# Weights of a pairwise bilinear kernel read as rows 248 KiB apart instead of contiguous blocks

## Chip, cores and metric

One core of one Trainium2 chip. The metric is device time in microseconds (us), as the median of repeated runs. KB in the profile's issue lists means 1024 bytes; the rows "254 KB apart" of the change are 253,952 bytes, 248 KiB.

## The reference

For each of the 496 pairs (i, j) of 32 fields, the vector of field i is multiplied by that pair's 128 x 128 matrix, and the result is multiplied element by element with field j.

```python
v_i = inputs[:, I_IDX, :]                 # [1024, 496, 128]
v_j = inputs[:, J_IDX, :]
transformed = jnp.einsum('bpd,ped->bpe', v_i, W)     # W: [496, 128, 128]
return transformed * v_j                  # 260 MB of float32
```

## The kernel before

Each pair has two halves of 512 batch columns. TensorE makes the product in PSUM. For all but the first 15 pairs it takes three float32r matmuls on split operands, with a scaling by ScalarE in between; ScalarE and GpSimd split the weights shortly ahead of use. VectorE multiplies by field j into one of four output buffers of two pairs each, and SyncE's queue stores the buffer as 1 MB with rows of 8 KB. The same queue loads weights, four pairs at a time, and x.

```python
WL = 4                      # pairs per weight load
WLEAD = 4                   # loads ahead
rpool = ctx.enter_context(tc.tile_pool(name="wr", bufs=5))     # raw weights
opool = ctx.enter_context(tc.tile_pool(name="o", bufs=4))      # output, 2 pairs each
...
def load_x(f, n=1, pieces=1, eng=None):
    ...
        (eng or nc.sync).dma_start(out=t[:, :, k * s : (k + 1) * s], in_=xt[:, f : f + n, k * s : (k + 1) * s])
...
def load_w(c, splits=(0, WL)):
    w_raw[c] = rpool.tile([P, WL, P], F32, tag="w", name=f"w_{c}")
    for a, b in zip(splits, splits[1:]):
        nc.sync.dma_start(out=w_raw[c][:, a:b, :], in_=wt[c, :, a:b, :])
...
for u in range(2 * NQ + LAG):           # half pairs
    q = u // 2
    if u % (2 * WL) == 0 and (q // WL + WLEAD) * WL < NQ:
        load_w(q // WL + WLEAD)
    ...                                  # matmuls of u, product and store of u - LAG, splits ahead
...
xt = _np.ascontiguousarray(x.transpose(2, 1, 0))                       # [d, field, b]
wt = _np.ascontiguousarray(w[perm].reshape(NQ // WL, WL, P, P).transpose(0, 3, 1, 2))
```

## Time and profile before

| | kernel before |
|---|---|
| time, median (first three runs) | 768.28 us (766.63 to 769.2) |
| span of the profiled run | 769.8 us |
| TensorE / ScalarE / VectorE / GpSimd busy | 722.7 / 638.7 / 632.0 / 593.2 us |
| DMA engines, main queue | 99.4% of 16 engines' span |
| output / x / weights moved | 260.0 / 16.8 / 32.5 MB |
| packets of 8 / 4 / 2 KB, main queue | 31,616 / 3,840 / 16,256 |

Read this table from the bottom. A DMA packet is here one row of one partition. If the recorded times of all packets, divided by 16, add up to the span, the engines have hardly any idle time, and then it is the packet count times the packet duration that must be asked about. The mean of a packet group minus its median is its tail: stalls of single packets. The lines themselves are in the prediction.

### The profile page before, as it was taken

To read this page: it belongs to the slowest core of one execution; us is meant where nothing else is said; L and a number is where in the kernel's file an instruction comes from. 1 tells how busy PE (TensorE), PEld (TensorE's weight loads), DVE (VectorE), ACT (ScalarE), POOL (GpSimd) and SP (SyncE) were. 2 spreads that over 40 slices of the span, in tenths; PEclk is the share of its full clock that TensorE was granted. 3 is DMA by queue.
4 is the path that set the end of the run, shared out by engine and by line. 5 is a ranking of instruction groups with operands and counts; after the bars stand their busy time and mean duration, and the time that the engine had idled before them with its cause. 6 is when DMAs were issued, how large, how long until landed. Compare 5 with 4: busy or idle time off the path is not lost.

```text
span 769.8 us, 11824 instructions
## 1 busy us (share of the span) xinstructions
PE 722.7 (94%) x2946; PEld 545.4 (71%) x2946; DVE 632.0 (82%) x1012; ACT 638.7 (83%) x1256; POOL 593.2 (77%) x863
## 2 busy tenths in 40 slices
PE   7988999999999999999999989999999999999994
PEld 3556766677777676777777767777777777777773
DVE  4869888888888788888888878888888888888885
ACT  2276988888888898888888889998988898998983
POOL 2677998887889878878878696978786969697660
PEclk9999999999999999999999999999999999999998
DMA  9999999999999999999999999999999999999997
GB/s 352 424 419 384 407 397 410 405 400 406 410 405 403 400 409 416 409 379 421 411 414 407 412 403 406 411 407 408 415 410 395 408 410 409 409 408 405 400 401 307
DMA packets 59108, 310.11 MB, mean 403 GB/s; under 512 B 6560, under 2 KB 6816, under 8 KB 27424
## 3 DMA queue, kind: packets, MB, share of 16 engines
q1 hardware_dynamic: 58464, 308.31, 99.4%
q10 hardware_dynamic: 576, 1.05, 0.4%
q8 instruction: 24, 0.39, 0.2%
q14 instruction: 44, 0.36, 0.1%
HBM read 49.28 MB, written 260.05 MB: 402 GB/s over the span
## 4 chain that ended last, share of the span: by engine, by line
DMA 61%; DVE 21%; PE 15%; issue 2%; DVEq 0%; SPq 0%; ACT 0%
DMA out_dram<-ot 60%; DVE ot L172 19%; PE po L157 9%; PE po L166 4%; DVE xd L195 2%; PE po L154 1%; DMA x<-in_xt_dram 1%; DVEq L172 0%; SPq L85 0%; DVEq L217 0%; ACT po L158 0%; DVEq L195 0%
## 5 line engine op out<-in xcount | busy, mean ns | idle before, releaser
L172 DVE TENSOR_TENSOR ot<-po,x 128x512 f32<-128x512 f32 x992 | 618.6, 684 | 129.5 <-DMA out_dram<-ot 70.2
L158 ACT ACTIVATE po<-po 128x512 f32<-128x512 f32 x962 | 551.2, 583 | 106.5 <-PE po L157 53.3
L157 PE MATMUL po<-xh,wh 128*128 128x512 f32 x962 | 388.7, 404 | 24.4 <-DVE ot L172 21.6
L166 PE MATMUL po<-xd,wd 128*128 128x512 f32 x962 | 376.9, 392 | 5.7 <-DVE xd L195 5.7
L157 PE MATMUL po<-xl,wl 128*128 128x512 f32 x962 | 377.6, 392 | 2.2 <-POOL wl L95 2.1
L157 PEld LDWEIGHTS po<-xh,wh 128*128 128x128 f32 x962 | 180.9, 188 | 110.2 <-DVE ot L172 72.5
L95 POOL TENSOR_TENSOR wl<-w,wh 128x256 fp32r<-128x256 f32 x241 | 179.2, 744 | 92.1 <-ACT wh L94 90.7
L166 PEld LDWEIGHTS po<-xd,wd 128*128 128x128 f32 x962 | 181.0, 188 | 46.3 <-ACT po L158 3.8
L157 PEld LDWEIGHTS po<-xl,wl 128*128 128x128 f32 x962 | 181.1, 188 | 36.8 <-POOL wl L95 4.5
L97 POOL TENSOR_TENSOR wd<-wl,wd 128x256 fp32r<-128x256 f32 x241 | 180.0, 747 | 20.1
L96 POOL TENSOR_SCALAR wd<-wh 128x256 fp32r<-128x256 f32 x241 | 99.1, 411 | 20.3
L94 ACT ACTIVATE wh<-w 128x256 fp32r<-128x256 f32 x241 | 99.2, 412 | 0.5 <-DMA w<-in_wt_dram 0.5
L110 POOL TENSOR_TENSOR xl<-x,xh 128x512 fp32r<-128x512 f32 x52 | 67.3, 1293 | 19.8 <-ACT xh L109 19.5
L115 POOL TENSOR_TENSOR xd<-xh,xl 128x512 fp32r<-128x512 f32 x32 | 41.4, 1292 | 2.7
L109 ACT ACTIVATE xh<-x 128x512 fp32r<-128x512 f32 x52 | 32.5, 628 | 10.5 <-DMA x<-in_xt_dram 10.3
L111 POOL TENSOR_SCALAR xl<-xl 128x512 fp32r<-128x512 f32 x52 | 32.8, 631 | 4.6
L154 PE MATMUL po<-x,w 128*128 128x512 f32 x60 | 29.0, 645 | 4.1 <-DMA x<-in_xt_dram 4.1
L154 PEld LDWEIGHTS po<-x,w 128*128 128x128 f32 x60 | 12.1, 206 | 20.2 <-issue 13.9
L195 DVE TENSOR_TENSOR xd<-xh,xl 128x512 fp32r<-128x512 f32 x20 | 16.6, 831 | 0.0
L109 ACT ACT_TABLE_LOAD x1 | 1.3, 1283 | 2.6 <-issue 2.6
L211 POOL MEMSET const-float32-0.0<- 128x1 f32 x1 | 0.1, 98 | 0.2 <-issue 0.2
L211 POOL MEMSET const-bfloat16-1.0<- 128x1 bf16 x1 | 0.1, 101 | 0.0
(2 smaller groups left out, 0.2 us busy)
## 6 DMA issues: line engine op xcount, KB each, us to landing
out_dram<-ot SPq DMA_DIRECT2D x247, 1024.0 KB, 8.9
w<-in_wt_dram SPq DMA_DIRECT2D x123, 256.0 KB, 9.1
x<-in_xt_dram SPq DMA_DIRECT2D x30, 512.0 KB, 9.5
x<-in_xt_dram ACTq DMA_DIRECT2D x4, 256.0 KB, 5.1
out_dram<-ot SPq DMA_DIRECT2D x4, 256.0 KB, 7.0
w<-in_wt_dram SPq DMA_DIRECT2D x1, 192.0 KB, 3.6
w<-in_wt_dram SPq DMA_DIRECT2D x1, 64.0 KB, 2.9
```

Of the source, the lines that this page charges most:

```text
L94: nc.scalar.mul(h, raw, 1.0 - 2.0**-13)
L95: nc.gpsimd.tensor_tensor(l, raw, h.bitcast(F32), ALU.subtract)
L96: nc.gpsimd.tensor_scalar(d, h.bitcast(F32), EPS, 1.0, ALU.mult, ALU.mult)
L97: nc.gpsimd.tensor_tensor(d, l.bitcast(F32), d.bitcast(F32), ALU.subtract)
L109: nc.scalar.mul(h, x_sb[f][:, s], 1.0 - 2.0**-13)
L110: nc.gpsimd.tensor_tensor(l, x_sb[f][:, s], h.bitcast(F32), ALU.subtract)
L115: nc.gpsimd.tensor_tensor(d, h.bitcast(F32), l.bitcast(F32), ALU.subtract)
L154: nc.tensor.matmul(po[u], w_raw[q // WL][:, q % WL, :], x_sb[i][:, s], start=True, stop=True)
L157: nc.tensor.matmul(po[u], w_s[c][t][:, r], x_s[i][t][:, s], start=t == 0, stop=t == 1)
L158: nc.scalar.mul(po[u], po[u], 1.0 + EPS)
L166: nc.tensor.matmul(po[u], w_s[q // WC][2][:, r], x_s[i][2][:, s], start=False, stop=True, skip_group_check=True)
L172: nc.vector.tensor_tensor(ots[g][:, k, s], po.pop(u), x_sb[j][:, s], ALU.mult)
```

## The change

The intent is a plain transposed layout [d, pair, e] on the host, in which a load may take any run of pairs. A load still takes four pairs, 2 KB per partition, but the 128 source rows, which lay end to end in 256 KB, now lie 248 KiB apart. The on-chip program keeps its order on all engines.

```diff
-            nc.sync.dma_start(out=w_raw[c][:, a:b, :], in_=wt[c, :, a:b, :])
+            nc.sync.dma_start(out=w_raw[c][:, a:b, :], in_=wt[:, c * WL + a : c * WL + b, :])
@@
-    wt = _np.ascontiguousarray(w[perm].reshape(NQ // WL, WL, P, P).transpose(0, 3, 1, 2))
+    wt = _np.ascontiguousarray(w[perm].transpose(2, 0, 1))
```

## The prediction

> **What bounds the kernel now.** I read the page's shares and slices first, then the queues, the chain of waits that ended last, a steady stretch of that chain, the waits, and last the single DMA packets of the trace, grouped by size. In the lines below, the slices give the busy tenths of the 16 DMA engines and what they moved.
>
> ```profile
> PE 722.7 (94%) x2946; PEld 545.4 (71%) x2946; DVE 632.0 (82%) x1012; ACT 638.7 (83%) x1256; POOL 593.2 (77%) x863
> ...
> DMA  9999999999999999999999999999999999999997
> ...
> q1 hardware_dynamic: 58464, 308.31, 99.4%
> ...
> HBM read 49.28 MB, written 260.05 MB: 402 GB/s over the span
> ...
> DMA 61%; DVE 21%; PE 15%; issue 2%; DVEq 0%; SPq 0%; ACT 0%
> ```
>
> TensorE looks busiest of the compute engines at 94%, but the DMA engines are full in every slice but the last, and one queue alone takes 99.4% of them. Of the 309 MB, 260 MB is output. The chain says the same: 61% of it is DMA, all but 1% the store of the output. A steady stretch of the chain shows how the kernel is paced:
>
> ```profile
> 589.45 8.95 DMA out_dram<-ot
> ...
> 598.52 2.50 DVE ot L172 x4
> ...
> 601.03 8.94 DMA out_dram<-ot
> ...
> 610.10 2.50 DVE ot L172 x4
> ```
>
> A store lands after 8.95 us, the output buffer is free, VectorE fills it with four products in 2.50 us, and it is stored again: one turn each 11.58 us (601.03 - 589.45). There are four such buffers, so one group of two pairs takes 11.58 / 4 = 2.90 us. Is that the DMA's own pace or mere latency? The packets answer. In the trace a packet of 8 KB (output rows) has a median of 309 ns, one of 4 KB (x rows) 159 ns, one of 2 KB (weight rows) 84 ns: 9 ns plus 75 ns for each 2 KB. The means are 319.7, 172.6 and 86.0 ns. A group's engine time is 8 output packets x 319.7 + 4 weight packets x 86.0 = 2558 + 344 = 2902 ns, which is the 2.90 us of the turn. And all packets of all queues add up to 770.4 us on each of 16 engines, against a span of 769.8. So the kernel is bound by DMA engine time: each nanosecond that a packet gets longer is paid in full.
>
> The loads of the weights themselves, and who waits for them:
>
> ```profile
> w<-in_wt_dram SPq DMA_DIRECT2D x123, 256.0 KB, 9.1
> ...
> x<-in_xt_dram SPq DMA_DIRECT2D x30, 512.0 KB, 9.5
> ```
>
> ```profile
> DVE ot L172 <- DMA out_dram<-ot: 70.2, 83, 2.1
> ...
> ACT wh L94 <- DMA w<-in_wt_dram: 0.5, 2, 0.3
> ```
>
> The last number of the first fence is the time from issue to landing in us; the waits are in total, times, longest. Nearly nobody waits for weights: 0.5 us in all. VectorE does wait for stores.
>
> **What the Trainium skill says.** "DMA: Bandwidth & Descriptors", section "Why a DMA increments its semaphore by 16 and not by 1": one descriptor moves one contiguous run of the last dimension, and a tile of 128 partitions is spread over 16 engines. The trace agrees: 123 weight loads of 256 KB make 123 x 128 = 15,744 packets of 2 KB, though the source was one contiguous block. Same page, "Latency and other measured facts", row on HBM row pitch at large powers of two: copies of [128 x 16 KiB] tiles ran at 207 GB/s per direction with a 512 KiB row pitch, 164 at 2 MiB, 103 at 4 MiB, and at 214 (called full) once the 4 MiB pitch was padded by 4 KiB; its mechanism, aliasing of HBM channels, is called an inference. The kernel before gives a partial test: x is already loaded as rows 128 KiB apart, a power of two. "HBM Reference", "Access": one core alone measures about 425 GB/s, bounded by its 16 DMA engines; here 8192 B in 309 ns on 16 engines is 424 GB/s. The same page, "Latency": 0.2 us on average and 2 us at high load; the longest 2 KB packet here took 1.63 us, so single slow reads exist.
>
> **The change part by part.** Removed: nothing that runs. The instruction order of all five engines is the same in both programs (the DMA queue's 405 entries too), and the built loads have the same destination, 128 rows of 512 elements; only the source step goes from 512 to 63,488 elements (253,952 B). The first block is still loaded in two pieces of 512 B and 1.5 KB rows. Packets: still 15,744 of 2 KB, because the destination was already cut by partition and the source row is still 2 KB. Bytes: the same 32.5 MB. Alignment: 253,952 is 31 x 8192, so rows still start on 8 KB steps plus the chunk's offset. Issue cost on the queue and TensorE, ScalarE, VectorE and GpSimd work: 0 us.
>
> Added: only what an HBM read of scattered rows costs over a contiguous read. Weight rows are 124 x 128 = 15,872, so 992 per engine; d ns more per row cost 992 x d / 1000 us. For d I have the x loads as a sample. Five of them (36 to 72 us) have a mean of exactly 159.0 ns, no penalty; the sixteen from 86 us on have means of 163 to 200 ns, on average about 182, so 23 ns over the median. Contiguous weight rows in the same trace are hardly ever slow: 225 of 16,768 packets of 2 KB (weights and a few pieces of x and output) took over 100 ns, and their whole excess is 2.0 us per engine. So pitched reads can cost something here. I choose a small d for the weights: 248 KiB isn't a power of two, it is 256 KiB less 8 KiB, which is the kind of pad that the skill says restores the full rate, and successive rows walk through 8 KiB steps, where x's rows differ only in bits from 128 KiB up. I take d = 2.5 ns: 992 x 2.5 = 2.5 us. Sum: 768.3 + 2.5 = 770.8 us, +0.3%.
>
> **The rivals.**
> (1) The weights behave like the later x rows: d = 23 ns, 992 x 23 = 22.8 us, about 791 us, 3% slower. For it: 23 ns was measured in this kernel, amid the same stores; and a weight row is only 2 KB, so each row has less to spread a miss over. Against: x's pitch is a power of two, and five x loads showed none of it.
> (2) Much worse: all rows of a load share the same address bits below 8 KiB, so if few channels serve them the reads might run at half speed: d = 84 ns, +83 us, about 850 us. Against it: x rows share even more of their low bits, and their median is unhurt.
> (3) The transfer is hidden: nothing is seen at all, about 768 us. A later landing alone would be hidden. A load is issued at the start of a block, four blocks of four pairs ahead; the split may run eleven pairs after the issue, 11 x 1.45 = 16 us, against 9.1 us to landing, 12.6 at the most. But engine time isn't hidden, as the engines are full; so this holds only with d near 0.
> (4) The stores suffer from scattered reads between them, beyond the weight packets' own time: 31,616 output packets, 1,976 per engine; 5 ns each would be 9.9 us. Against it: output packets in the time of x loads had means of 310 to 349 ns, around the overall 319.7, with no clear surplus.
> (5) Faster: their 8 KB packets have 10.7 ns of mean excess, 21 us per engine, which a lucky spread of reads could lower. Nothing in the profile points to it; 2% would need 15 of those 21 us.
>
> **Range and chances.** Runs of the kernel before spread over 766.6 to 769.2. The low end, 765, is (3) with that spread and a microsecond or so of (5). The high end, 783, is d of about 15 ns, between my choice and (1). Slower by over 2% begins at 783.6 us, d = 15.4 ns: I give (1), (2) and (4) 0.11 together. Faster by over 2% means under 752.9: 0.01. Within 2%: 0.88. **Predicted: 770.8 us, 765 to 783.**
>
> **What would show it.** In the profile after: the same packet counts (16,256 of 2 KB on the main queue) with a median of 84 ns shows the descriptors unchanged; the mean of 2 KB packets at 86 to 90 ns shows d, and at 105 or more shows rival (1). DMA share still 99% or so; the sum of all packets over 16 engines equal to the span again. The wait of ScalarE for weights stays under 2 us in all, else the lead was too short. Output packets' mean stays within 317 to 324 ns, else (4). The chain's turn in the steady stretch stays 11.5 to 11.8 us. The prediction is wrong if the median itself moves, if the row count changes, or if slow packets gather at the weights or the stores.

## The result

The changed kernel took 768.69 us (767.3 to 770.82, 6 runs) against 768.05 us (765.79 to 769.46, 6 runs) for the kernel before. The ratio is 1.0012, with a 95% interval of 0.9991 to 1.0034: the same. A ratio here is the mean time of one kernel's runs over the mean of the other's runs of the same rounds, so it is not quite the ratio of the medians quoted beside it. Executions over 1.5% slower than the fastest of the same kernel are left out of the means.

From the page of the changed kernel: the DMA engines' slices, the queue that carries the load, and the bytes:

```profile
DMA  9999999999999999999999999999999999999997
...
q1 hardware_dynamic: 58464, 308.31, 99.4%
...
HBM read 49.28 MB, written 260.05 MB: 403 GB/s over the span
```

The packet count of the main queue is the one of before, to the packet, and so is its share. A steady stretch of the changed kernel's chain (start in us, duration, what):

```profile
603.69 8.99 DMA out_dram<-ot
...
612.80 2.49 DVE ot L172 x4
...
615.31 8.96 DMA out_dram<-ot
```

The turn of an output buffer is 615.31 - 603.69 = 11.62 us, against 11.58 before. Not every turn is so steady: over the whole span the chain goes through TensorE and GpSimd a little more than before, where it was 61% DMA and 15% TensorE:

```profile
DMA 57%; DVE 19%; PE 18%; POOL 2%; issue 2%; DVEq 0%; ACT 0%; SPq 0%; POOLq 0%
```

Last, the page's issues (KB each, median us from issue to landing), and the waits for DMA (us in total, times, longest):

```profile
w<-in_wt_dram SPq DMA_DIRECT2D x123, 256.0 KB, 9.1
x<-in_xt_dram SPq DMA_DIRECT2D x30, 512.0 KB, 9.4
```

```profile
DVE ot L172 <- DMA out_dram<-ot: 73.0, 80, 3.0
...
ACT wh L94 <- DMA w<-in_wt_dram: 0.5, 2, 0.3
```

Scattered weight loads land in the same 9.1 us, and ScalarE waits for them the same 0.5 us. The packets of the two traces, main queue:

| packets | median before, after | mean before | mean after |
|---|---|---|---|
| 2 KB (weights, 512 others) | 84, 84 ns | 86.0 ns | 86.6 ns |
| 4 KB (x) | 159, 159 ns | 172.6 ns | 172.5 ns |
| 8 KB (output) | 309, 309 ns | 319.7 ns | 318.1 ns |
| all queues, sum over 16 engines | | 770.4 us | 767.9 us |

The 2 KB packets got 0.6 ns longer in the mean. The single profiled run after happens to be 3 us shorter than the one before, through 1.6 ns less per output packet. The timed runs show no such gain.

### The profile page after: what moved, and what is told of

The parts are those of the page before. It is cut to its first block, busy times and chain, and to the rows that moved or that the text cites. A ratio compares the mean times of both kernels' runs of the same rounds, so it can differ in the third digit from the quotient of the medians.

```text
span 766.8 us, 11824 instructions
## 1 busy us (share of the span) xinstructions
PE 717.7 (94%) x2946; PEld 548.1 (71%) x2946; DVE 632.5 (82%) x1012; ACT 635.1 (83%) x1256; POOL 595.1 (78%) x863
## 4 chain that ended last, share of the span: by engine, by line
DMA 57%; DVE 19%; PE 18%; POOL 2%; issue 2%; DVEq 0%; ACT 0%; SPq 0%; POOLq 0%
DMA out_dram<-ot 56%; DVE ot L172 18%; PE po L157 11%; PE po L166 5%; PE po L154 2%; DMA x<-in_xt_dram 1%; DVE xd L195 1%; POOL wl L95 1%; POOL xd L115 1%; POOL xl L110 0%; POOL xl L111 0%; DVEq L172 0%; POOL wd L97 0%; POOL wd L96 0%; SPq L85 0%
## 5 line engine op out<-in xcount | busy, mean ns | idle before, releaser
L97 POOL TENSOR_TENSOR wd<-wl,wd 128x256 fp32r<-128x256 f32 x241 | 181.3, 752 | 20.1
```

Source lines behind the costliest of these rows:

```text
L97: nc.gpsimd.tensor_tensor(d, l.bitcast(F32), d.bitcast(F32), ALU.subtract)
```

## The experiments

Two questions were left. Is it the pitch of 248 KiB that is harmless, or any pitch? And is the DMA really where a longer packet would be paid, so that "no effect" means "no cost" and not "hidden"? All kernels below derive from the changed one and are timed against the kernel before.

| run | what | time (us) | ratio to before, 95% interval | 2 KB mean | 8 KB mean |
|---|---|---|---|---|---|
| w_pitch256k | rows 256 KiB apart | 768.74 | 1.0028 (0.9984 to 1.0073) | 86.9 ns | 317.3 ns |
| w_pitch2m | rows 2 MiB apart | 872.22 | 1.1340 (1.1271 to 1.1409) | 103.1 ns | 355.9 ns |
| w_rows512 | four 512 B rows for one of 2 KB | 779.38 | 1.0158 (1.0122 to 1.0194) | - | 318.0 ns |
| w_none | 119 of 124 loads gone (wrong result) | 733.09 | 0.9556 (0.9515 to 0.9598) | - | 321.3 ns |
| w_skip4 | 29 of 124 loads gone (wrong result) | 750.78 | 0.9750 (0.9708 to 0.9792) | 86.6 ns | 317.6 ns |
| w_twice | 54 loads more | 802.70 | 1.0436 (1.0382 to 1.0489) | 85.2 ns | 318.5 ns |
| x_pad4k | x rows 132 KiB apart | 770.21 | 1.0009 (0.9979 to 1.0039) | 85.5 ns | 319.2 ns |
| w_rows4k | eight pairs per load | 773.69 | 1.0065 (1.0033 to 1.0096) | - | 316.0 ns |
| w_rows4k_xpad | both of the last two | 774.80 | 1.0063 (1.0026 to 1.0100) | - | 316.4 ns |
| w_rows4k_late | eight pairs, issued later | 776.76 | 1.0076 (1.0026 to 1.0125) | - | 321.9 ns |

### Other pitches

```diff
-    wt = _np.ascontiguousarray(w[perm].transpose(2, 0, 1))
+    wt = _np.zeros((P, 512, P), _np.float32)        # 4096 in w_pitch2m
+    wt[:, :NQ, :] = w[perm].transpose(2, 0, 1)
```

> The changed kernel with the pair axis of the weights padded from 496 to 512, so rows lie 256 KiB apart, a power of two, instead of 248 KiB. Theory of the prediction (power-of-two pitch costs, 248 KiB does not): the mean of the 2 KB packets rises from 86.6 to about 107 ns (as the later x rows, 23 ns over the median) and the time by about 20 us to 790, ratio 1.02 to 1.04. Rival (the pitch as such costs nothing at 2 KB rows, and the slow x rows have another cause): mean 86 to 88 ns, ratio 0.997 to 1.004.

> The same with the pair axis padded to 4096, rows 2 MiB apart. The skill's row gives 164 GB/s at 2 MiB against 214 with a padded pitch, 30% more time. If the same holds for 2 KB rows: mean of the 2 KB packets about 110 ns or more (84 x 1.3), about 24 us more, ratio 1.03 at least; if the penalty is per row (373 ns for a 16 KiB row by the skill's two rates), several hundred us more. Rival (2 KB rows among nine times as many store bytes hide it): mean below 90 ns, ratio 1.00 to 1.005.

At 256 KiB nothing happened: 86.9 ns, ratio within noise of 1. The theory that 248 KiB is harmless because it isn't a power of two falls, as a power of two next to it costs nothing measurable either.

At 2 MiB the kernel is 13% slower. Its chain, and its waits for DMA:

```profile
DMA 70%; DVE 22%; PE 5%; issue 1%; DVEq 0%; ACT 0%; SPq 0%
DMA out_dram<-ot 69%; DVE ot L172 21%; PE po L157 3%; PE po L166 2%; DVE xd L195 1%; DMA w<-in_wt_dram 1%; DMA x<-in_xt_dram 1%; DVEq L172 0%; ACT po L158 0%; DVEq L218 0%; SPq L76 0%; SPq L85 0%; DVEq L195 0%
```

```profile
DVE ot L172 <- DMA out_dram<-ot: 170.5, 109, 3.4
...
ACT wh L94 <- DMA w<-in_wt_dram: 1.3, 2, 1.0
```

The damage does not show where the change is: the wait for weights is 1.3 us, while VectorE's wait for stores rises from 73.0 to 170.5 us. Per engine, the 2 KB packets take 104.8 us against 88.0 in the changed kernel (+16.8), and the stores, whose code was not touched, 703.3 against 628.6 (+74.7). The expectation from the skill's two rates was right in that the pitch costs, but it was too high for the weight packets (103 ns, where 110 or more was expected) and too low for the time, as most of the recorded cost fell on the transfers in between. All packets together rose from 767.9 to 858.9 us per engine, by 91, and the time by 13.4% of 768, that is 103 us: what the packets got longer was paid in full. The sum ends 12 us short of the span of 870.6 us, so idle DMA time came on top.

Is it the loads that hurt the stores, or does the output merely lie elsewhere in DRAM beside a tensor of 268 MB? The trace can tell. In the 100 us before the last weight packet landed, the stores took 365 ns in the mean, and 17% of them over 340 ns; in the 20 us after it, 316 ns, and 0.3%. So they are slow only while these loads run. Where between 256 KiB and 2 MiB the cost begins was not measured, nor whether rows 2 MiB and a few KiB apart would be free; so it isn't shown that the power of two is to blame and not the size.

### Is packet time paid?

w_rows512 cuts the weight rows to 512 B:

```diff
-            nc.sync.dma_start(..., in_=wt[:, c * WL + a : c * WL + b, :])
+            nc.sync.dma_start(..., in_=wt[c * WL + a : c * WL + b].rearrange("q d e -> d q e"))
@@
-    wt = _np.ascontiguousarray(w[perm].transpose(2, 0, 1))
+    wt = _np.ascontiguousarray(w[perm].transpose(0, 2, 1))
```

> The weights laid out as [pair, d, e], so each weight row of a load is four runs of 512 B. Tests that engine time of weight packets is paid in full. 63,488 packets of 512 B instead of 15,872 rows of 2 KB; the few 512 B packets of the traces took 25 to 27 ns in the median, 29.6 in the mean. Theory (paid in full): four of them take 108 to 118 ns against 86, so 992 rows per engine x 22 to 32 ns = 22 to 32 us more, 790 to 801 us, ratio 1.028 to 1.042. Rival (weight loads are hidden, small costs vanish): ratio 0.998 to 1.004, with the packets longer all the same.

The 512 B packets took 27.4 ns in the mean, four of them 109 ns, as expected, and the sum of all packets rose from 767.9 to 790.3 us, by 22.4. But the time rose by 1.58% of 768, that is 12 us, with an interval of 9 to 15. The queue line of this kernel tells why the sum isn't the time here:

```profile
q1 hardware_dynamic: 105952, 308.31, 100.9%
```

One queue's packets take more than the engines' whole span, so their records overlap. For these packets, about 10 of the 22 us recorded were not paid.

Two kernels change the number of packets and not their kind. w_skip4 takes every fourth weight block from the eighth on from the one before, 29 blocks (its expectation below says 30; the trace has 3,712 packets fewer, which is 29 x 128); w_twice loads 54 blocks a second time into buffers of x that are still idle.

```diff
     def load_w(c, splits=(0, WL)):
+        if c >= 5 and c % 4 == 0:             # w_skip4 alone
+            w_raw[c] = w_raw[c - 1]
+            return
```

```diff
+    spare = {}
+
     def load_w(c, splits=(0, WL)):
+        if 5 <= c < 59:                       # w_twice alone
+            f, k = c % 6 // 2, c % 2 * WL
+            if f not in spare:
+                spare[f] = xpool.tile([P, 2 * WL, P], F32, tag=f"x{f}", name=f"spare_{f}")
+            nc.sync.dma_start(out=spare[f][:, k : k + WL, :], in_=wt[:, c * WL : (c + 1) * WL, :])
```

> Wrong result on purpose: of the blocks from the eighth on, every fourth is not loaded and takes the block before it; 30 of 124 loads vanish, 30 x 8 x 86.6 ns = 20.8 us per engine. Theory A (DMA bound until TensorE takes over near 733 us, where the kernel without weight loads ended): 768 - 21 = 747 us, ratio 0.972 to 0.978. Theory B (DMA and TensorE share the bound already at 768, each waits for the other at times): a part only, about 757 to 762 us, ratio 0.984 to 0.993, as 82 us fewer gave only 33.

> The changed kernel; 54 of the 124 weight blocks are loaded a second time into SBUF that lies idle until late x loads need it, and never read. The result stays right. Doses the DMA upward in packets of the same kind: 54 x 8 x 86.6 ns = 37.4 us of time on each engine. Theory A (the DMA is the bound, upward every nanosecond is paid): 768 + 37 = 805 us, ratio 1.049 (1.042 to 1.055). Theory B (recorded packet times overlap, as 512 B rows suggested, where 22 us more of them cost 12 us): about half, 787 us, ratio 1.02 to 1.03.

The 2 KB packets of w_skip4 took 67.9 us per engine in its trace against 88.0, so 20.1 us less; the time fell by 2.50% of 768, 19.2 us (16 to 22). Those of w_twice took 123.4 us, 35.4 more; the time rose by 4.36%, 33.5 us (29 to 38). In both directions some 95% of the dose was paid, and the intervals hold the whole of it. This is Theory A of both expectations; sharing of the bound by half is excluded. The queue and the chain of w_skip4, then of w_twice:

```profile
q1 hardware_dynamic: 54288, 300.70, 99.0%
...
PE 60%; DMA 24%; DVE 9%; POOL 4%; issue 1%; ACT 0%; SPq 0%; DVEq 0%; POOLq 0%; ACTq 0%
```

```profile
q1 hardware_dynamic: 66240, 322.47, 100.0%
...
DMA 59%; PE 21%; DVE 16%; issue 1%; POOL 1%; DVEq 0%; ACTq 0%; SPq 0%; POOLq 0%
```

The chain of w_skip4 runs mostly through TensorE, although the DMA dose was paid: 19 us below the kernel, the two bounds are already close.

w_none takes the dose to its end:

```diff
     def load_w(c, splits=(0, WL)):
+        if c >= 5:
+            w_raw[c] = w_raw[c - 5]
+            return
```

> Wrong result on purpose: only the first five weight blocks are loaded, all later blocks reuse them, so 119 of 124 loads vanish. Theory (DMA engine time is the bound all the way): 119 x 8 rows per engine x 86.6 ns = 82 us less, 686 us, ratio 0.893. Rival (another engine is the bound soon below): TensorE's busy time is 718 us in the profile, ScalarE's 635; the time would stop near 720 to 750, ratio 0.94 to 0.975, and the DMA share fall below 97%.

Here the rival held. The time fell by 34 us (4.44% of 768) where 82 were taken off the DMA. The page says what stopped it:

```profile
PE 692.1 (95%) x2946; PEld 552.4 (76%) x2946; DVE 683.4 (94%) x1012; ACT 625.8 (86%) x1256; POOL 594.2 (81%) x863
...
q1 hardware_dynamic: 41328, 277.10, 93.9%
...
PE 85%; POOL 7%; DVE 3%; DMA 2%; issue 1%; ACT 0%; SPq 0%; DVEq 0%; POOLq 0%
```

The chain is 85% TensorE and 2% DMA. So the next bound lies 34 us below the present one: TensorE's matmuls with the work of the other engines between them. VectorE, at 94% busy, is close to it as well. In the kernel with all loads the DMA is the bound, but the next one isn't far.

### What made some x rows slow

The prediction took its worst rival from the x rows, which take 23 ns over the median from about 86 us on. (Times of packets, here and in the prediction, count from the zero of the packet records, which lies 11 us before the start of the profile's span; there it is 75 us.) Two kernels ask whether that was the pitch or the address. x_pad4k adds one unused field row to x; x_swap16 exchanges fields 0 to 15 with 16 to 31 in DRAM alone.

```diff
-    xt = _np.ascontiguousarray(x.transpose(2, 1, 0))
+    xt = _np.zeros((P, NF + 1, BT), _np.float32)      # x_pad4k
+    xt[:, :NF, :] = x.transpose(2, 1, 0)
```

```diff
-    ..., in_=xt[:, f : f + n, ...]
+    ..., in_=xt[:, (f + 16) % NF : (f + 16) % NF + n, ...]      # x_swap16
@@
-    xt = _np.ascontiguousarray(x.transpose(2, 1, 0))
+    roll = (_np.arange(NF) + 16) % NF
+    xt = _np.ascontiguousarray(x[:, roll, :].transpose(2, 1, 0))
```

> The changed kernel with one more field row in x's DRAM layout, so x rows are 132 KiB apart instead of 128 KiB. Theory (the slow x rows come from the power-of-two pitch): the mean of the 4 KB packets falls from 172.5 to 159 to 163 ns, 3840/16 x 10 to 13 ns = 2.3 to 3.2 us less, ratio 0.996 to 0.998. Rival (they come from what else runs from 80 us on, or from reads scattered over rows as such): mean stays 168 to 176 ns, ratio 0.999 to 1.002.

> The changed kernel with fields 0 to 15 and 16 to 31 exchanged in DRAM, the order of the loads in time kept. The five x loads between 36 and 75 us are clean (159 to 161 ns in the mean) and lie at offsets of 64 KiB and more within a pitch; the sixteen slow ones after 80 us lie below 64 KiB. If the address decides: the five early loads turn slow (175 to 200 ns) and the sixteen late ones clean (159 to 163). If the time decides: early ones stay at 159 to 161, late ones at 167 to 202.

With rows 132 KiB apart the x packets took 171.0 ns in the mean against 172.5, and the time did not move: it wasn't the power of two. With the fields swapped, the five early loads stayed clean (159.0 to 161.1 ns), and fourteen of the sixteen late ones stayed slow (170 to 196 ns; the first and the last of them were at 159.7 and 161.5): it wasn't the address either. In w_none, with hardly any weight loads, the x packets still took 171.5 ns, so it isn't the weights.

### Rows of 4 KB, and a try at a faster kernel

The new layout allows a load to take eight pairs, so rows of 4 KB. To fit, the raw weights get two buffers of 4 KB in place of five of 2 KB, and the first two blocks lie in buffers of x that are used late.

```diff
-WL = 4
+WL = 8
-WLEAD = 4
+WLEAD = 2
-    rpool = ctx.enter_context(tc.tile_pool(name="wr", bufs=5))
+    rpool = ctx.enter_context(tc.tile_pool(name="wr", bufs=2))
@@
-        w_raw[c] = rpool.tile([P, WL, P], F32, tag="w", name=f"w_{c}")
+        if splits[0] == 0:
+            pool, tag = (xpool, f"x{c}") if c < 2 else (rpool, "w")
+            w_raw[c] = pool.tile([P, WL, P], F32, tag=tag, name=f"w_{c}")
... (the first loads are cut to match)
-        if u % (2 * WL) == 0 and (q // WL + WLEAD) * WL < NQ:
+        if u % (2 * WL) == 4 and (q // WL + WLEAD) * WL < NQ:      # == 8 in w_rows4k_late
```

> The changed layout lets a load take eight pairs as one run: 62 loads of 4 KB rows instead of 124 of 2 KB. Theory (9 ns fixed per packet plus 75 ns per 2 KB, paid in full): a 4 KB packet takes 159 ns instead of 2 x 84, so 496 rows per engine x 9 ns = 4.5 us less, about 764 us, ratio 0.994 (0.991 to 0.997). Rival A (nothing gained since the loads are hidden): 0.999 to 1.001. Rival B (the larger loads come in bigger lumps and hold up the stores, or come too late with two buffers): slower, ratio 1.002 to 1.01, with waits of ScalarE for weights of several us.

> Both: eight pairs per load and x rows 132 KiB apart. Theory: 4.5 us for the packets and 2.3 to 3.2 us for x, together 7 us, about 761 us, ratio 0.991 (0.987 to 0.995). Rival: only one or none of the two counts, 0.994 to 1.001.

Both were slower than before, by 0.65% and 0.63%; x's padding adds nothing, as above. Two things went against the theory. First, the expected saving of 9 ns per pair of rows isn't there: the median of a 4 KB packet is 159 ns, but the mean over weights and x is 175 ns, against 2 x 86.6 = 173. In the stretch from 470 to 720 us, where only weights come in 4 KB packets, it is 174 ns: the tail of the x rows turns up on weight rows as soon as these are 4 KB long. Second, the queue's own waits of w_rows4k:

```profile
SPq L87 <- POOL wl L97: 104.9, 41, 5.8
SPq L87 <- POOL wd L98: 9.9, 12, 1.1
```

With a third such line of 4.3 us, SyncE's queue stood for 119 us before a weight load until GpSimd had let go of one of the two raw buffers, with stores queued behind. In the changed kernel these waits for GpSimd are 82 us in all, most of it in three lines:

```profile
SPq L85 <- POOL wd L97: 32.5, 36, 1.3
SPq L85 <- POOL wd L96: 24.2, 42, 1.6
SPq L85 <- POOL wl L95: 14.6, 12, 1.6
```

(The next expectation compares the wl lines alone, 105 with 15 us.) w_rows4k_late issues two pairs later, to take away this wait.

> As w_rows4k, the loads issued two pairs later. There the DMA queue stood 105 us waiting for GpSimd to release one of the two raw weight buffers, against 15 us in the changed kernel, while stores queued behind. Theory (that wait is what made it 0.65% slower): the wait falls below 20 us, and with packets of 175 ns in place of 2 x 86.6 there is nothing left to gain or lose: ratio 0.996 to 1.002. Rival (4 KB weight rows in lumps of 512 KB are themselves the cause): the wait falls and the time stays, ratio 1.004 to 1.010.

```profile
SPq L87 <- POOL wl L97: 18.1, 14, 3.0
...
SPq L87 <- POOL wd L98: 15.9, 24, 1.2
```

```profile
ACT wh L96 <- DMA w<-in_wt_dram: 11.6, 11, 7.1
```

The waits for GpSimd went down to 45 us in all, below those of the changed kernel, and the time did not come back (1.0076). So that wait alone isn't the cause. In its place ScalarE now waits 11.6 us for weights that land too late. The sums of all packets show where the loss lies: 764.7 us in w_rows4k, 766.3 in w_rows4k_xpad and 772.6 in w_rows4k_late, against spans of 769.8, 773.8 and 778.5. They fall 5 to 8 us short of the span, where those of the changed kernel reach it (767.9 of 766.8). In the first two the packets take less time in sum than in the changed kernel; so these profiled runs are longer because the DMA engines stand idle more, and not because packets got longer. Whether the waits or the larger lumps leave them idle is open; with two buffers an earlier issue waits for the buffer and a later one for the data. No version beat the kernel before.

w_rows4k_block is the same with contiguous blocks of eight pairs:

```diff
-in_=wt[:, c * WL + a : c * WL + b, :]
+in_=wt[c, :, a:b, :]
@@
-    wt = _np.ascontiguousarray(w[perm].transpose(2, 0, 1))
+    wt = _np.ascontiguousarray(w[perm].reshape(NQ // WL, WL, P, P).transpose(0, 3, 1, 2))
```

> As w_rows4k_late, with the weights as contiguous blocks of eight pairs as in the kernel before. Between 470 and 720 us only weights are read in packets of 4 KB; with rows 248 KiB apart these took 174 to 180 ns in the mean, median 159. If the row length decides (the tail belongs to reads of 4 KB): 172 to 182 ns again. If scattered rows decide: 159 to 164 ns.

In the same stretch its 4 KB weight packets took 170 ns in the mean, against 172 (late), 174 (w_rows4k) and 179 (w_rows4k_xpad) for scattered rows, medians all 159. Single groups of 128 packets in this stretch, some 21 in each kernel, have means from 159 to 242 ns, so these four are not clearly apart. That is between the two expectations, nearer to the first: contiguous 4 KB rows have most of the tail as well, 11 of the 13 to 20 ns. The tail goes with the 4 KB packet more than with the pitch. One rival is left: 4 KB rows always came in loads of 512 KB, 2 KB rows in 256 KB. In w_twice two loads of 2 KB rows were issued 0.6 to 2.2 us apart, 512 KB together, without such a tail (85.2 ns), which speaks against it and isn't proof. The cause of the tail, and why x loads before about 80 us lack it, stay open.

## Why the prediction was right

It said 770.8 us and "within 2%", and 768.69 was measured.

- **The bound.** That DMA engine time is paid in full holds for packets of an unchanged kind: 95% of the dose in w_skip4 and w_twice. Longer packets were paid too: all of the 91 us at 2 MiB. It has two limits that the prediction did not name: downward it ends after 34 us, where TensorE takes over (w_none), and with 512 B packets only 12 of 22 us were paid, as their records overlap. The sum of 770.4 us in a span of 769.8, on which the prediction rested this step, didn't prove it; the doses do.
- **The parts removed and unchanged.** Same packet counts, medians and wait of ScalarE for weights: as told.
- **The term d.** 2.5 ns was chosen, 0.6 ns measured, 0.6 us in 992 rows per engine. Other runs with the same 248 KiB rows had means of 85.2 to 86.6 ns around the 86.0 of before, so d can't be told from zero.
- **The reason given for a small d.** This was the weak step. The prediction argued that 248 KiB isn't a power of two and acts like a padded pitch. w_pitch256k shows that a power of two of nearly that size is free too. And the sample for the worst case, the later x rows, did not measure a pitch at all: padding x changed nothing, and 4 KB weight rows have the tail even when contiguous. So rival (1) had less for it than it seemed. The skill's row, on which the argument leaned, begins at 512 KiB and pads a pitch of 4 MiB; 8 KiB less than 256 KiB isn't in it. That d came out near zero although this reason for it was not the right one is luck in this step; what makes pitches up to 256 KiB free stays open.
- **Rival (4), harm to the stores.** It is absent at 248 KiB (318.1 ns) and is the main cost at 2 MiB (355.9 ns). The mechanism exists; the dose was not reached.
- **Rivals (2), (3) and (5).** The median did not move, against (2). Doses of weight packets were paid, so (3) is right in its number, but the transfer is not hidden. As for (5), the profiled run's output packets were 1.6 ns shorter, but the ratio shows no gain.
- **A citation.** The 425 GB/s of "HBM Reference" stands there in "Specifications (TRN2)".

## What to carry to other kernels

Before fearing a strided load, ask whether the number and length of its packets change: here the destination cuts 256 KB into 128 rows of 2 KB in either layout, and rows 248 or 256 KiB apart cost nothing that could be measured, while four 512 B rows for each 2 KB row cost 1.6%. If a very large pitch does cost, look for the damage in other transfers' packets too, as here at 2 MiB, and not only in the wait for the load itself. And test a claimed bound in both directions with packets of the same kind: one step down and one up showed that DMA time is paid in this kernel, and one large step down showed where it ceases to be.

## What the Trainium skill lacked or had wrong

- "DMA: Bandwidth & Descriptors", "Latency and other measured facts", row on HBM row pitch at large powers of two: the row speaks of [128 x 16 KiB] copies alone. Here, with 2 KB rows among stores, 256 KiB was free (ratio 1.0028), 2 MiB cost 13%, and of the added packet time at 2 MiB 74.7 us per engine fell on contiguous stores and only 16.8 us on the strided loads. That a large pitch harms other traffic isn't stated there.
- Same row: 512 KiB is the least pitch that it gives, and it doesn't say from which pitch on its advice to pad by a few KiB is worth following. For x rows of 4 KB, 4 KiB more on 128 KiB changed nothing (172.5 to 171.0 ns in the mean, ratio 1.0009).
- Same page, "Specifications", gives 512 B as the least transfer for line rate. In this kernel 512 B packets took 27.4 ns, four of them 109 ns against 86.6 for one of 2 KB (of these 22 ns about 12 were paid), and the kernel was 1.6% slower.
- No page tells of the tail of 4 KB load packets (median 159 ns, mean 169 to 176 over weights and x), which takes away most or all of the gain over two 2 KB packets (2 x 86.6 ns), nor warns that recorded packet times can add up to more than the span (100.9% of it on one queue in w_rows512).
